# Loading the first image first, and layers 1 to 3's constants beside layer 0's first work, in a four-layer convolution and attention kernel

## The chip, the cores and the metric

The kernel runs on one core of a Trainium2 chip. A core has five engines, each with its own instruction queue: TensorE (PE in the profile; PEld is its weight load), VectorE (DVE), ScalarE (ACT), GpSimd (POOL) and SyncE (SP), which here only issues DMAs. They wait for each other through semaphores, and each engine takes its instructions strictly in the order in which they were written. The metric is the device time of one execution over a batch of 32 images, in microseconds (us). Less is better.

## The reference

Input `x` is 32 images of 56 x 56 pixels with 96 channels, float32. Four layers follow each other:

```python
# layer 0: a conditional bottleneck; rw are 4 gates per image
rw = sigmoid(mean(x, (1, 2)) @ Wr + br)
h = relu(bn(x @ einsum('be,ecm->bcm', rw, Wpw) + rw @ bpw))      # 96 -> 384 channels
h = relu(bn(sum_e rw[e] * (depthwise3x3(h, Wdw[e]) + bdw[e])))
x = bn(h @ einsum('be,emf->bmf', rw, Wpwl) + rw @ bpwl) + x      # 384 -> 96
# layer 1
x = x + depthwise5x5(x, kernel)
# layer 2
x = bn(depthwise3x3(relu(x), dw) @ pw + pw_bias)
# layer 3: shifted 7x7 window attention (3 heads) and a perceptron with gelu
x = x + attention(layernorm(x)) @ wo + bo
x = x + gelu(layernorm(x) @ w1 + b1) @ w2 + b2
```

The gates need the mean over the whole image, so nothing of layer 0 can start before its image is in SBUF, its sum is taken and the router (`rw`) has run.

## The kernel before

Line numbers are those of the kernel before, as its profile has them.

**Stages.** Each image passes four stages. `stage_router` loads the image (`xT`, 96 channels on partitions x 3136 pixels), sums it in two halves on ScalarE (`sums`, through the accumulator), makes `pooled` and `pooled_w` on VectorE, multiplies by `wr` on TensorE, and makes `rw` and the mixed weights `wmix`, `wmix2` and `mix`. `stage_conditional` is layer 0's main part: for each of four strips of 14 rows and three blocks of 128 channels it expands on TensorE, evicts on ScalarE to `h1`, and takes nine taps of the 3 x 3 depthwise convolution into `h2` (printed as `h`): the first on ScalarE, eight on VectorE, as SCALAR_TENSOR_TENSOR of 128 x 784. Then a ReLU on ScalarE, the projection on TensorE, its eviction to `y` (two buffers) on ScalarE, and the residual addition `xT <- y, xT` on GpSimd. `stage_depthwise` is layers 1 and 2 as banded matmuls with `band5`, `band3` and `pw`. `stage_swin` is layer 3.

**The order of the work.** The stages don't issue instructions. A `Recorder` notes each as a `Work` with a cost, what it waits for, and a target time. `Recorder.order` then plans the whole run with a small list of costs: at each moment a free engine takes the work with the earliest target whose inputs are ready and whose buffers (`Ring`) are free. `give` writes the instructions in that order; this is why nearly all of them carry line 488. Where TensorE would idle for longer than `SPARE_AFTER` (250 ns) and a bank is free, the planner puts in a filler: a 128 x 128 matmul of `ident` with itself (`banks<-ident` in the profile; each float32 matmul is two rows there). Image 0's and image 1's stages overlap, so the routers of both are near the start; the plan has ScalarE sum the first halves of image 0 and of image 1, and then the second halves.

**The constants.** Ahead of the planned work, written in the plain order of the program, stand:

- `scratch` (536): pieces of `h2`'s first buffer, used as room for small constants. `mhalves` (552) is one, filled with -0.5.
- `rsqrt` (557, 558): a VectorE instruction adds epsilon, and GpSimd raises to the power -0.5.
- layer 0's loads (562, 570, 583, 601), their transposition on TensorE (587, 604), and batch-norm constants `s1`, `s2`, `s3` (558, 615 to 617).
- `band5` and the six additions of `centre` to it (640), `band3`, `pw`.
- layer 2's batch norm of 128 x 96 pieces: `inv2` by `rsqrt`, then 654 and 660 to 665, which fold it into `pw`. 660 reads the bank that the matmul of 658 wrote.
- `centre_outputs` (670 to 672) for `pw` and `wo`, and 685.
- layer 3's loads, and memsets on GpSimd (699 to 712), among them the zero borders of `slots`, `kT`, `exps`, `x1`, `x2` and `h1`.

SyncE issues all of these loads before the first planned instruction, the load of image 0. In the built program each DMA issue waits for the landing of the one issued eight places before it.

Of the kernel before, what the change touches and what calls it, by code (L numbers as in the profile page):

```python
# [19 lines left out]
C = 96  # L20
CM = C + 1
M = 384
# [238 lines left out]
class Recorder:  # L261
# [77 lines left out]
    def order(self):  # L339
# [66 lines left out]
        def begin(w):  # L406
            nonlocal count
            for b in w.needs:
                if b.slot is None:
                    b.ring.free.sort()  # L410
                    b.slot = b.ring.free.pop(0)[1]
                    b.ring.begun += 1
            result.append(w)
            w.start = now
            e = w.engine
            if e == "gpsimd" or w.calls[0][0] == "scalar_tensor_tensor":
                running[e] = {"work": w, "left": w.ns, "since": now, "rate": 1.0}
                share(now)
                return
            free[e] = now + w.ns  # L420
            heapq.heappush(events, (free[e], count, None))
            heapq.heappush(events, (free[e] + w.landing, count + 1, w))
            count += 2
            if e == "tensor":
                heapq.heappush(events, (free[e] + SPARE_AFTER, count, None))
                count += 1

        left = len(self.work)
        spares = 0
        while left:  # L430
            for e in self.ENGINES:
                if free[e] > now:
# [2 lines left out]
                while queues[e]:  # L435
# [5 lines left out]
                    begin(w)  # L441
                    left -= 1
                    if e == "tensor":
                        spares = 0
                    break
                else:
                    if e == "tensor" and self.spare and now >= free[e] + SPARE_AFTER and self.spare[2].free:
                        lhs, rhs, ring = self.spare
                        w = Work(e, 0.0)
                        b = Buffer(ring)  # L450
                        operands = View(b, ring.tiles[0])[:, : rhs.shape[1]], lhs, rhs
                        w.calls.append(("matmul", operands, {"start": True, "stop": True}))
                        w.ns = cost(e, "matmul", operands, {})
                        w.needs, w.starts, w.uses, w.writes = [b], [b], [b], [b]
                        b.users[w], b.left, b.owner = True, 1, w
                        spares += 1
                        assert spares < 10000, "no work can start"
                        begin(w)
# [20 lines left out]
                count += 1  # L479
        return result  # L480

    def give(self, tc):
        with tc.manual_schedule():
            for w in self.order():
                for method, args, kw in w.calls:
                    args = [v.found() if isinstance(v, View) else v for v in args]
                    kw = {k: v.found() if isinstance(v, View) else v for k, v in kw.items()}
# [4 lines left out]
def kernel(  # L492
# [37 lines left out]
    if general:  # L530
# [2 lines left out]
        tops = ring("top", [PK, NP], 4)  # L533
        dens = ring("den", [PK, NP], 4)


    room = h2s.tiles[0].rearrange("p k n -> p (k n)")
    taken = [0]

    def scratch(rows, n):  # L540
        taken[0] += n
        return room[:rows, taken[0] - n : taken[0]]


    ident = const.tile([P, P], F32, name="ident")
# [2 lines left out]
    nc.gpsimd.memset(ones, 1.0)  # L548
    mhalf = const.tile([P, 4], F32, name="mhalf")
    nc.gpsimd.memset(mhalf, -0.5)  # L550
    mhalves = scratch(P, C)
    nc.gpsimd.memset(mhalves, -0.5)

    def rsqrt(dst, src, eps, scale=1.0):
# [75 lines left out]
    nc.vector.tensor_copy(experts[:, :, 9, :], c384[:, :, V_BPW : V_BPW + E])  # L630
    nc.vector.tensor_copy(experts[:, :, 10, :], c384[:, :, V_BDW : V_BDW + E])


    band5 = load([P, NG, 10, 32], layouts["k5"], "band5")
    centre = scratch(P, 64).rearrange("p (n c) -> p n c", n=2)
    nc.sync.dma_start(out=centre, in_=layouts["centre"])
    for g in range(NG):
        for n in range(2):
            at = 5 * n + 2
            nc.vector.tensor_tensor(band5[:, g, at], band5[:, g, at], centre[:, n], ALU.add)  # L640
    band3 = load([P, NG, 6, 32], layouts["k3"], "band3")


    pw = const.tile([C + 1, CM], F32, name="pw")
    nc.sync.dma_start(out=pw[:C, :C], in_=a["L2_conv_pw_kernel"].rearrange("a b c f -> (a b c) f"))

    def wide(name, keep=False):
        t = const.tile([P, C], F32, name=name) if keep else scratch(P, C)
        nc.sync.dma_start(out=t, in_=a[name].partition_broadcast(P))
        return t  # L650

    inv2 = wide("L2_conv_moving_var")
    rsqrt(inv2, inv2, BN_EPS)
    nc.vector.tensor_tensor(inv2, inv2, wide("L2_conv_gamma"), ALU.mult)
    dwb = scratch(C, P)
    nc.vector.tensor_scalar(dwb, ones[:C].to_broadcast([C, P]), col(U_DWB), None, ALU.mult)
    pt = mm.tiles[4]
    nc.tensor.matmul(pt[:, :C], dwb, pw[:C, :C], start=True, stop=True)
    bias2 = scratch(P, C)
    nc.vector.tensor_tensor(bias2, pt[:, :C], wide("L2_conv_pw_bias"), ALU.add)  # L660
    nc.vector.tensor_tensor(bias2, bias2, wide("L2_conv_moving_mean"), ALU.subtract)
    nc.vector.tensor_tensor(bias2, bias2, inv2, ALU.mult)
    nc.vector.tensor_tensor(bias2, bias2, wide("L2_conv_beta"), ALU.add)
    nc.vector.tensor_tensor(pw[:C, :C], pw[:C, :C], inv2[:C], ALU.mult)
    nc.vector.tensor_copy(pw[C:, :C], bias2[C : C + 1])

    def centre_outputs(w):

# [2 lines left out]
        nc.vector.tensor_scalar(mean, mean, 1.0 / C, None, ALU.mult)  # L671
        nc.vector.tensor_scalar(w[:, :C], w[:, :C], mean, None, ALU.subtract)

    centre_outputs(pw)


    wq = load([C, C], a["L3_conv_wq"], "wq")
    wk = load([C, C], a["L3_conv_wk"], "wk")
    wv = load([C, C], a["L3_conv_wv"], "wv")
    wo = const.tile([C + 1, CM], F32, name="wo")  # L680
    nc.sync.dma_start(out=wo[:C, :C], in_=a["L3_conv_wo"])
    nc.sync.dma_start(out=wo[C:, :C], in_=a["L3_conv_bo"].rearrange("(o c) -> o c", o=1))
    centre_outputs(wo)
    if not general:
        nc.vector.tensor_scalar(wo[:C], wo[:C], -1.0, None, ALU.mult)
    w1 = load([C, M], a["L3_conv_w1"], "w1")
    w2 = load([P, NB, C], a["L3_conv_w2"].rearrange("(k p) f -> p k f", p=P), "w2")
    b2 = wide("L3_conv_b2", True)
    if general:
        masks = load([PK, 2, NP * PK], layouts["mask"].rearrange("l q j k -> q l (j k)"), "masks")  # L690
    else:
        keep_last = load([P, NP, WT], layouts["keep_last"], "keep_last")
        keep_column = load([P, WT], layouts["keep_column"], "keep_column")

        slots = ring("slots", [C, NWIN, SLOT], 3)

        exps = ring("exps", [P, NH, NP, PK], 2)
        for t in slots.tiles + kTs.tiles + exps.tiles:
            nc.gpsimd.memset(t, 0.0)
        ones32 = const.tile([P, HD], F32, name="ones32")  # L700
        nc.gpsimd.memset(ones32, 1.0)

    for t in x1s.tiles + x2s.tiles + [h1.tiles[0] for h1 in h1s]:
        nc.gpsimd.memset(t, 0.0)
    for t in filtereds.tiles + oTs.tiles:
        nc.gpsimd.memset(t[C:], 1.0)

    for t in lnsqs.tiles:
        nc.gpsimd.memset(t[:, :, C:], C * LN_EPS)
    for u in (U_LN1G, U_LN2G):
        nc.vector.tensor_scalar(col(u), col(u), math.sqrt(C), None, ALU.mult)

# [12 lines left out]
    def stage_router(b):  # L728

        xT = chip.new(xTs).part(*range(NROW))  # L730
        sums = new_small("sums", [C, 2])
        chip.sync.dma_start(out=xT, in_=x[b])
        yield 3
        for q in range(2):
            part = xT[:, q * HALF * W : (q + 1) * HALF * W].part(*range(4 * q, 4 * q + 4))
# [733 lines left out]
    for step in range(B + 3):  # L1469
# [11 lines left out]
        if step < B:  # L1481
            stages.append((stage_router(step), 12, when("router", step)))
        interleave(stages)
    chip.give(tc)


def build(nc, shapes, batch):
# [41 lines left out]
```

## Time and profile before

| what | us |
|---|---|
| median of 3 runs | 5219.56 (5214.7 to 5220.35) |
| the profiled execution, its own time | 5218.23 |
| its span, first to last instruction | 5216.4 |
| TensorE busy | 5044.7 (97%) |
| VectorE busy | 4300.9 (82%) |
| images 0 and 1: DMAs issued from | 29.19 |
| first sum on image 0, on image 1 | 37.10, 41.65 |
| first router matmul | 53.08 |
| first tap on VectorE | 62.36 |
| TensorE busy from 0 to 10, 20 to 30, 30 to 40 us | 0.96, 1.60, 0.00 |
| DMA rate from 20 to 30, 30 to 40 us | 157, 251 GB/s |

The time between the profiled execution's span and its own time (1.8 us) is what lies around the first and last instruction. A line of the timeline gives the start in us from the span's start, the duration (from the first to the last where several like instructions are merged, with their count), the engine, the line, the operation and its tiles, and in brackets how long the engine was idle before and what ended that. Buffer numbers are left out of the names, so `h` stands for `h1` and `h2` alike, and for the small constants that borrow `h2`'s room. SPq lines are DMA issues, not transfers. Lines of the chain of waits give start, duration and who held the chain.

### The profile page before, as it was taken

The page shows a single profiled execution, that of the slowest core. Times are in us where ns is not written, and L with a number is a line of the kernel's source. Part 1 is how long each engine was busy: PE and PEld are TensorE (multiplying, and loading weights), DVE is VectorE, ACT ScalarE, POOL GpSimd, SP SyncE. Part 2 cuts the span into 40 slices and gives each one's busy share as a digit, 9 for nine tenths or more (in the row PEclk, how much of TensorE's full clock was granted, in tenths as well). Part 3 has the DMA queues.
Part 4 walks back from the last instruction along what each step waited for, and adds up shares of the span by engine and source line. Part 5 has one row for each costly group of instructions (what it writes and reads, how often), then busy time and mean ns, then how long its engine had stood idle before and what let it go on. Part 6 is the DMA issues. An engine that isn't in the chain of part 4 may idle for free.

```text
span 5216.4 us, 139773 instructions
## 1 busy us (share of the span) xinstructions
PE 5044.7 (97%) x58652; PEld 3347.7 (64%) x58652; DVE 4300.9 (82%) x5560; ACT 3841.3 (74%) x7649; POOL 3041.9 (58%) x2432
## 2 busy tenths in 40 slices
PE   5889999999999999999999999999999999999999
PEld 3556666666666666666666666666666666666677
DVE  6887988888988888988888888888888888898722
ACT  2457787777778777777877777877777877777755
POOL 5456755565765555666465665656566555566533
PEclk9899999999999999999999999999999999999999
DMA  1111111111111111101111111111111111110110
GB/s 43 22 27 39 23 28 33 37 36 38 31 25 31 33 39 36 39 20 29 35 37 36 38 27 27 32 36 37 37 34 23 32 33 39 36 39 20 24 28 19
DMA packets 482579, 166.35 MB, mean 32 GB/s; under 512 B 477952, under 2 KB 478613, under 8 KB 478869
## 3 DMA queue, kind: packets, MB, share of 16 engines
q1 hardware_dynamic: 481940, 157.33, 14.7%
q8 instruction: 464, 7.60, 0.6%
q14 instruction: 175, 1.43, 0.1%
HBM read 41.60 MB, written 38.54 MB: 15 GB/s over the span
## 4 chain that ended last, share of the span: by engine, by line
PE 74%; POOL 9%; DVE 6%; ACT 5%; issue 5%; DMA 1%; SPq 0%; DVEq 0%; POOLq 0%; ACTq 0%
PE banks L488 74%; DVE h L488 4%; POOL tb L488 3%; POOL lnd L488 2%; ACT exps L488 2%; POOL xT L488 2%; POOL exps L488 1%; POOL var L488 1%; ACT h L488 1%; ACT hid L488 1%; DVE hid L488 1%; DVE wmix L488 1%; DMA out<-tb 1%; ACT slots L488 0%; DVE res L488 0%
## 5 line engine op out<-in xcount | busy, mean ns | idle before, releaser
L488 DVE SCALAR_TENSOR_TENSOR h<-h,mix,h 128x784 f32<-128x784 f32 x3072 | 3309.9, 1113 | 71.7 <-ACT h L488 56.5
L488 POOL TENSOR_TENSOR var<-var,mhalf 112x4 f32<-112x4 f32 (+1 forms) x512 | 775.4, 1520 | 418.9 <-DVE var L488 409.8
L488 PE MATMUL banks<-x,band 32*32 32x392 f32 x24576 | 851.1, 508 | 0.0
L488 POOL TENSOR_TENSOR xT<-y,xT 96x392 f32<-96x392 f32 x256 | 480.6, 1879 | 491.8 <-ACT y L488 490.5
L488 PE MATMUL banks<-xT,wmix 96*128 96x448 f32 (+1 forms) x1536 | 693.7, 550 | 1.4 <-issue 1.4
L488 ACT ACTIVATE h<-h,biasd,s 128x784 f32<-128x784 f32 x384 | 399.0, 1039 | 348.8 <-DVE h L488 348.6
L488 ACT ACTIVATE hid<-banks,c 128x448 f32<-128x448 f32 (+1 forms) x768 | 437.0, 583 | 287.9 <-PE banks L488 279.5
L488 PEld LDWEIGHTS banks<-w,hid 128*112 128x112 f32 x5376 | 579.9, 182 | 82.0 <-issue 37.8
L488 POOL TENSOR_TENSOR tb<-res 112x384 f32<-112x384 f32 (+1 forms) x256 | 459.8, 1801 | 282.7 <-DMA out<-tb 181.2
L488 PE MATMUL banks<-hT,w 96*128 96x448 f32 (+1 forms) x1536 | 615.5, 502 | 0.2 <-DVE tb L488 0.2
L488 POOL TENSOR_TENSOR lnd<-res,var 112x384 f32<-112x384 f32 (+1 forms) x512 | 590.3, 1159 | 32.8 <-PE banks L488 16.2
L488 ACT ACTIVATE h<-banks,bias,s 128x448 f32<-128x448 f32 (+1 forms) x768 | 539.4, 710 | 90.8 <-PE banks L488 85.0
L488 PE MATMUL banks<-w,hid 128*112 128x96 f32 x5376 | 588.4, 266 | 7.4 <-ACT hid L488 6.4
L488 PE MATMUL banks<-h,wmix 128*96 128x392 f32 x1536 | 560.2, 503 | 17.0 <-ACT h L488 17.0
L488 PEld LDWEIGHTS banks<-x,band 32*32 32x32 f32 x24576 | 407.8, 103 | 247.0 <-issue 161.7
L488 ACT ACTIVATE exps<-banks 49x196 f32<-49x196 f32 x1536 | 507.8, 331 | 40.5 <-PE banks L488 15.8
L488 POOL TENSOR_TENSOR exps<-exps,keep_column 49x147 f32<-49x147 f32 x224 | 207.2, 925 | 479.3 <-ACT exps L488 443.8
L488 PEld LDWEIGHTS banks<-h,wmix 128*96 128x96 f32 x1536 | 245.1, 166 | 258.9 <-issue 210.3
L488 PEld LDWEIGHTS banks<-xT,wmix 96*128 96x128 f32 x1536 | 259.2, 191 | 199.8 <-issue 95.0
L488 ACT ACTIVATE h<-h,mix 128x784 f32<-128x784 f32 x384 | 364.5, 949 | 29.3 <-POOL h L488 21.1
L488 DVE TENSOR_REDUCE var<-lnsq 112x4 f32<-112x388 f32 (+1 forms) x512 | 253.1, 497 | 159.7 <-POOL lnd L488 120.0
L488 PEld LDWEIGHTS banks<-hT,w 96*128 96x128 f32 x1536 | 256.4, 190 | 144.9 <-issue 73.3
(131 smaller groups left out, 7499.6 us busy)
## 6 DMA issues: line engine op xcount, KB each, us to landing
xT<-in_x SPq DMA_DIRECT2D x32, 1176.0 KB
x<-xT SPq DMA_DIRECT2D x384, 98.0 KB
out<-tb SPq DMA_DIRECT2D x128, 168.0 KB
filtered<-x SPq DMA_DIRECT2D x384, 49.0 KB
filtered<-x SPq DMA_DIRECT2D x384, 42.0 KB
out<-tb SPq DMA_DIRECT2D x128, 126.0 KB
filtered<-x SPq DMA_DIRECT2D x384, 7.0 KB
wpw<-in_L_conv_Wpw SPq DMA_DIRECT2D x1, 576.0 KB
```

What stands on the lines that cost most here:

```text
L488: getattr(getattr(self.nc, w.engine), method)(*args, **kw)
```

## The change

- Image 0's load is written ahead of all other loads of the kernel; in the plan an entry without instructions (`brought`) stands in its place. Image 1's load stays planned, and now follows layer 0's constants and `pw`.
- The loads of layers 1 to 3 are held back. `give` writes three groups between the planned instructions, each ahead of the first instruction that the plan starts at 15, 45 or 85 us: `first_others` (18 loads, and the memsets of layers 1 to 3), `more_others` (the `rsqrt` of `inv2`) and `last_others` (the `band5` additions, layer 2's folding, `centre_outputs`).
- The small constants of layers 1 to 3, and `mhalves`, lie in the room of `x3` instead of `h2`'s first buffer. The matmul for `bias2` stays ahead; a copy now takes it out of its bank at once.
- The planner puts in no filler before the first planned matmul. 37 fillers go.

```diff
+        begun = False
...
                     if e == "tensor":
-                        spares = 0
+                        spares, begun = 0, True
...
-                    if e == "tensor" and self.spare and now >= free[e] + SPARE_AFTER and self.spare[2].free:
+                    if e == "tensor" and begun and self.spare and now >= free[e] + SPARE_AFTER and self.spare[2].free:
...
+    def brought(self, v):
+        w = Work("sync", self.target)
+        w.ns, w.landing = COST["sync", "dma_start"][0], IMAGE_LANDING
+        self.work.append(w)
+        self.touch(w, v, True)
...
-    def give(self, tc):
+    def give(self, tc, others):
+        others = sorted(others.items(), reverse=True)
         with tc.manual_schedule():
             for w in self.order():
+                while others and w.start >= others[-1][0]:
+                    others.pop()[1]()
...
+    nc.sync.dma_start(out=xTs.tiles[0], in_=x[0])
+    rooms = [h2s.tiles[0].rearrange("p k n -> p (k n)"), x3s.tiles[0].rearrange("p g m w -> p (g m w)")]
...
-    mhalves = scratch(P, C)
+    mhalves = scratch(P, C, 1)
...
+    bias2 = scratch(P, C, 1)
+    nc.vector.tensor_copy(bias2, pt[:, :C])
...
+    def first_others():
+        for t, src in held:
+            nc.sync.dma_start(out=t, in_=src)
+        if not general:
+            for t in slots.tiles + kTs.tiles + exps.tiles:
+                nc.gpsimd.memset(t, 0.0)
+            nc.gpsimd.memset(ones32, 1.0)
+        for t in x1s.tiles + x2s.tiles:
+            nc.gpsimd.memset(t, 0.0)
+        for t in filtereds.tiles + oTs.tiles:
+            nc.gpsimd.memset(t[C:], 1.0)
+        for t in lnsqs.tiles:
+            nc.gpsimd.memset(t[:, :, C:], C * LN_EPS)
+
+    def more_others():
+        rsqrt(inv2, inv2, BN_EPS)
...
+    def last_others():
+        for g in range(NG):
+            for n in range(2):
+                at = 5 * n + 2
+                nc.vector.tensor_tensor(band5[:, g, at], band5[:, g, at], centre[:, n], ALU.add)
+        nc.vector.tensor_tensor(inv2, inv2, gamma2, ALU.mult)
+        nc.vector.tensor_tensor(bias2, bias2, pwb2, ALU.add)
+        nc.vector.tensor_tensor(bias2, bias2, mean2, ALU.subtract)
+        nc.vector.tensor_tensor(bias2, bias2, inv2, ALU.mult)
+        nc.vector.tensor_tensor(bias2, bias2, beta2, ALU.add)
+        nc.vector.tensor_tensor(pw[:C, :C], pw[:C, :C], inv2[:C], ALU.mult)
+        nc.vector.tensor_copy(pw[C:, :C], bias2[C : C + 1])
+        centre_outputs(pw)
+        centre_outputs(wo)
+        if not general:
+            nc.vector.tensor_scalar(wo[:C], wo[:C], -1.0, None, ALU.mult)
+
+    others = {15000: first_others, 45000: more_others, 85000: last_others}
...
-        chip.sync.dma_start(out=xT, in_=x[b])
+        if b:
+            chip.sync.dma_start(out=xT, in_=x[b])
+        else:
+            chip.brought(xT)
...
-    chip.give(tc)
+    chip.give(tc, others)
```

In the built program of after, VectorE has the addition of epsilon to `inv2` (557 before) after the 12th tap of image 0, and `last_others` after the 49th. GpSimd has the memsets of `first_others` ahead of the power for `s1`, and the power for `inv2` behind all of these and ahead of the first residual addition. SyncE has image 0, layer 0's loads, `pw`, image 1, the 18 held loads.

## The prediction

> **What bounds the kernel now.** I read the page first (busy shares, slices), then the chain that ended last, then VectorE, ScalarE, GpSimd and SyncE in order of time over the first 340 us, where every line of the diff acts.
>
> The page says that TensorE fills the span, except in its first slice:
>
> ```profile
> span 5216.4 us, 139773 instructions
> PE 5044.7 (97%) x58652; PEld 3347.7 (64%) x58652; DVE 4300.9 (82%) x5560; ACT 3841.3 (74%) x7649; POOL 3041.9 (58%) x2432
> ```
>
> The middle of the run can't change: stripped of the fillers, TensorE's order in the two built programs is the same, and the banks differ by one fixed renaming; so are ScalarE's, VectorE's and GpSimd's orders, apart from the first 140 instructions or so. 37 fillers go. Nothing later is replanned, so a time won or lost before image 0 has filled the pipeline should arrive whole at the end.
>
> In order of time, before the first multiply-add of the depthwise taps (columns: start, duration, engine, line, operation, idle before it and what ended it):
>
> ```profile
> 13.93 0.22 SPq L583 DMA_DIRECT2D h<-in_L_conv_b  x1
> 18.74 0.36 SPq L562 DMA_DIRECT2D band<-in_k  x1
> 27.05 15.68 POOL L558 TENSOR_TENSOR h<-h 128x96 f32<-128x96 f32 x1 [1.06 <-DVE h L557]
> 29.19 0.90 SPq L488 DMA_DIRECT2D xT<-in_x  x2
> 41.65 1.51 ACT L488 ACTIVATE xT<-xT 96x1568 f32<-96x1568 f32 x1 [2.95 <-DMA xT<-in_x]
> 46.05 0.19 ACT L488 ACTIVATION_READ_ACCUMULATOR xT<-xT 96x1 f32 x1
> ...
> 42.76 0.26 DVE L654 TENSOR_TENSOR h<-h 128x96 f32<-128x96 f32 x1 [15.80 <-POOL h L558]
> 43.59 9.65 PE L488 MATMUL banks<-ident 128*128 128x128 f32 x66 [19.15 <-DVE h L660]
> 53.08 0.28 PE L488 MATMUL banks<-wr,pooled_w 96*128 96x4 f32 x2
> 53.60 0.15 DVE L488 TENSOR_TENSOR rw<-banks,br 128x4 f32<-128x4 f32 x1
> 62.36 63.71 DVE L488 SCALAR_TENSOR_TENSOR h<-h,mix,h 128x784 f32<-128x784 f32 x67
> ```
>
> Both images are issued last, at 29.19. The power of layer 2's variance holds GpSimd 15.68 us; its reader L660 holds a bank, and 33 fillers (66 rows) stand before the router's matmul until 53.08. From 62.36 VectorE is the bound: 67 taps with no pause.
>
> Then the chain, and VectorE after the 67 taps:
>
> ```profile
> 94.06 32.89 POOL xT L488
> 126.97 0.69 ACT y L488
> ```
>
> ```profile
> 134.86 15.22 DVE L488 SCALAR_TENSOR_TENSOR h<-h,mix,h 128x784 f32<-128x784 f32 x16 [8.78 <-ACT h L488]
> ```
>
> An addition on GpSimd that takes 1.0 us alone (the next three, from 126.95) lasted 32.89 us beside uninterrupted taps. ScalarE's third `y` waited for it, the following taps got no input, and VectorE stood for 8.78 us. GpSimd instructions that read get no turn inside a tight row of taps. This row decides the case, since the change puts the 15.68 us power into that row of taps.
>
> **Part 1, first image first: the second image still decides.** ScalarE's order stays: first half of image 0, first half of image 1, then the second halves. VectorE takes both sums before `rw`. So the router's start hangs on image 1, which stands behind layer 0's constants on SyncE. The ninth DMA issue waits for the first: before, the issues paused from 10.2 to 13.93 for `wpw` and `wpwl`. Now image 0 (1176 KB at the 251 GB/s of the window 30 to 40: 4.8 us) is ahead of these. Issued at 5.77, 1.9 us later its bytes move (estimate; `wpw` took about that), so it ends near 12.5 and the four `wpwl` land about 18.0 instead of 13.93: all later issues move by 4.07. Image 1 stands one DMA (`pw`, 0.45) behind the place of `band` (18.74): 18.74 + 4.07 + 0.45 = 23.3. With 1.0 to the first byte, 4.8 of bytes and 1.8 from last byte to semaphore (bytes ended at 39.8, the sum began at 41.65) it lands at 30.9 instead of 41.65: 10.75 us won. Bounds: 29.0 (no shift of 4.07, partly made up by a slower load) to 32.5 (bytes shared with the bands behind it).
>
> **Part 2, the constants moved off the router's way.** The sums take 4.59 us from image 1's landing (41.65 to 46.24), now 30.9 to 35.5; a reduction, a product (0.14, 0.28) and `rw` is at 35.9. Before, `rw` came 7.36 after the last sum, since 33 fillers were queued; now 0.4. That wins 6.95. Together 53.60 becomes 35.9, **-17.7**. Layer 0's own constants are ready in time: GpSimd's memsets (slots to `filtered`, `oT`) now stand ahead of `s1`'s power, by their rows (5.8 to 25.6 before) they end near 22; the powers (1.73 and 0.55) then end near 25.6, VectorE's rest near 26.6, 8 us before the first sum is read. The 18 held DMAs, 0.47 us each, stand behind image 1 and land before 45; nobody reads them before 90.
>
> **Part 3, fillers.** Their 9.65 us are in the 6.95 already. What they may leave is a cold TensorE: the first twenty rows of the 66 went at 213 ns, the rest at 112, and cold expansion rows took 0.75 us instead of 0.375 (3.19 us for four at 77.33, 1.67 at 68.42). Now router, 3 fillers, router, 10 fillers run without a pause for some 5 us before the expansions, longer than the 4.3 us the twenty rows took. I take 0; the bound is 4 rows, +1.5. The Trainium skill (TensorE: Matmul & The Clock Gate, Part 1) says activity of some 3.4 to 4 us releases the half rate, which agrees; by it too the sum has 0 here.
>
> **Part 4, VectorE's constant work inside the taps.** After 12 taps comes L557's sum with epsilon (0.20), after 49 taps the six band additions (0.70) and then L654 to L685's fifteen instructions (42.76 to 46.33: 3.57). Before, they lay under the wait for the image and the fillers; now they are in the bound engine's row: **+4.5**.
>
> **Part 5, the power of 96 columns.** It is queued on GpSimd after the 12th tap, some 12 us into the row. L654 follows the 49th tap, 35 us later, so on paper 15.7 are hidden in 35. But it reads, and that row of taps gave an addition nothing for 32.89 us. I take it as held until the first break, the band additions, after which VectorE stands in front of L654 for all of it: **+15.7**. The other end is 0, if it gets in after the 12th tap and needs the port only for moments. For 0 speaks a trace record: at 342.29 a power of four columns got in between two taps and the next tap lasted 1.035 us, not stretched; so it doesn't hold the port while it computes, for four columns. Nearest to our place is the row at 94.06 (same engine pair, same kind of taps), so I take the full price. The Trainium skill (SBUF — State Buffer, Who interferes with whom) has it that an instruction of VectorE with two SBUF inputs and a reading one of GpSimd lock each other out, the first for its whole duration. By that rule even an early entry would stop the taps for 15.7, and the price is the same either way; by the four-column row an early entry costs nothing. The rule speaks against the change, and the row at 94.06 is on its side.
>
> **Part 6, the 8.78 us pause.** While VectorE stands for the power, GpSimd is free; the additions queued behind it follow during the 3.57 us of small instructions. `y` number three is then released near 108, and the taps 50 to 67 (17.0 us) cover the 7.9 us that ScalarE needed from 126.97 to the next start. So the old pause is filled: **-8.8** (bounds -8.8 and 0).
>
> **Sum:** -17.7 + 4.5 + 15.7 - 8.8 = **-6.3 us**. The profiled execution took 5218.23 (span 5216.4): 5211.9. The median of the three runs is 5219.56, 1.3 above it: 5213. About 0.2% (10.4 us) is what a measurement of this kernel can tell from no change, so this is within it.
>
> **Rivals.**
> - *The power gets its port early.* Taps and power run side by side: -17.7 + 4.5 - 8.8 = -22.0; if a later addition then starves and gives a pause of 8.8 back, -13.2. For it: the four-column record, and an addition at 179.02 that got in after one tap. Against: five additions before 340 us starved 16 to 33 us. 5197 to 5206.
> - *The old pause stays behind the new one (slower).* If the four additions don't get through during the small instructions, which have two SBUF inputs too, the row of taps 50 to 67 starves them again, and the 8.78 us remain: -17.7 + 4.5 + 15.7 = +2.5; where the additions of the next strip starve once more for want of a break, another 8.8: +11.3, to 5231. It decides from the point where the taps restart before the second addition has ended. Against: three additions took 2.9 us, in 3.57.
> - *The start doesn't reach the end.* TensorE is 97% busy; if another wait before 570 us (VectorE stood 16.5 us at 346 for a matmul) has slack that swallows the gain, nothing is left: 5219. Against: that wait is on work in the same order, which comes earlier too.
>
> **How the numbers follow.** The forecast (-2 to -10): 0.66; early port (-13 to -22): 0.18; old pause stays: 0.11; no effect: 0.05. Faster by over 0.2% is the early port and the lucky end of the forecast (image 1 at 29): 0.26. Slower by over 0.2%: a third of the second rival, 0.04, and 0.02 for what I don't see: 0.06. The rest, 0.68, is within. The likeliest case's own range is 5209 to 5218. For 8 in 10 I go down to 5198, which leaves out only the early port's end, and up to 5222, which leaves out the doubled pause.
>
> **What would show it.** `rw`'s first addition near 35.9 and the first tap near 44.7; image 1's sum beginning near 30.9; one GpSimd power lasting 40 to 55 us instead of 15.7, and VectorE standing some 15 us ahead of the second small product; no 8.8 us pause after tap 67; tap 68 near 128.6 (was 134.86). I am wrong if the power lasts about 16 us with taps going on, or if a pause of 8 us or more follows tap 67.

## The result, and the profile after

The changed kernel takes 5202.26 us in the median of 7 runs (5199.32 to 5214.36), against 5220.2 for the kernel before (median of 7, beside it). The ratio is 0.9971, with a 95% interval of 0.9961 to 0.9981: 0.29% faster, 18 us. The forecast was 5213, a change inside 0.2%; the time lies in the given range of 5198 to 5222, but in the part of it that the first rival named. The profiled execution of after was one of its longer ones (5214.36), at a granted clock of 0.985 instead of the 0.987 or 0.988 of those near the median: its lead over the profile of before stays near 15 us up to some 900 us of the span (15.5 at 929) and melts slowly from there (3.9 at the last tap), so I read the start, where every line of the diff acts, and take the end from the medians.

The page of after, its span and busy shares:

```profile
span 5212.6 us, 139630 instructions
PE 5050.6 (97%) x58578; PEld 3343.9 (64%) x58578; DVE 4300.9 (83%) x5561; ACT 3836.9 (74%) x7649; POOL 3028.8 (58%) x2432
```

74 matmul rows fewer (37 fillers), and one VectorE instruction more, the copy of `bias2`. The way to the first tap, from the timelines of SyncE, ScalarE, TensorE and VectorE of after (start, duration, engine, line, operation; the planned work now has line 500):

```profile
5.63 0.32 SPq L548 DMA_DIRECT2D xT<-in_x  x1
13.34 0.27 SPq L597 DMA_DIRECT2D h<-in_L_conv_bpw  x1
23.27 0.42 SPq L500 DMA_DIRECT2D xT<-in_x  x1
31.40 1.51 ACT L500 ACTIVATE xT<-xT 96x1568 f32<-96x1568 f32 x1 [16.38 <-DMA xT<-in_x]
35.05 0.59 PE L500 MATMUL banks<-wr,pooled_w 96*128 96x4 f32 x2 [9.23 <-DVE pooled_w L500]
36.48 0.15 DVE L500 TENSOR_TENSOR rw<-banks,br 128x4 f32<-128x4 f32 x1
45.31 11.69 DVE L500 SCALAR_TENSOR_TENSOR h<-h,mix,h 128x784 f32<-128x784 f32 x12
```

Image 1 is issued at 23.27, and ScalarE, which had nothing to do for 16.38 us, begins its sum at 31.40 (41.65 before). The router's matmul waits for nothing but `pooled_w`, and the first tap is at 45.31 instead of 62.36. Then what decided the case, the 96-column power and its surroundings on GpSimd and VectorE:

```profile
56.92 0.20 DVE L571 TENSOR_SCALAR x<-x 128x96 f32<-128x96 f32 x1
57.04 35.21 DVE L500 SCALAR_TENSOR_TENSOR h<-h,mix,h 128x784 f32<-128x784 f32 x37
57.20 16.40 POOL L572 TENSOR_TENSOR x<-x 128x96 f32<-128x96 f32 x1 [31.76 <-DVE x L571]
77.26 16.83 POOL L500 TENSOR_TENSOR xT<-y,xT 96x392 f32<-96x392 f32 x2 [3.66 <-ACT y L500]
92.18 2.37 DVE L730 TENSOR_TENSOR band<-band,x 128x32 f32<-128x32 f32 x6
94.47 0.24 DVE L731 TENSOR_TENSOR x<-x 128x96 f32<-128x96 f32 x1
97.77 26.56 DVE L500 SCALAR_TENSOR_TENSOR h<-h,mix,h 128x784 f32<-128x784 f32 x28
126.29 6.52 DVE L500 SCALAR_TENSOR_TENSOR h<-h,mix,h 128x784 f32<-128x784 f32 x6 [1.96 <-POOL h L500]
155.83 35.78 POOL L500 TENSOR_TENSOR xT<-y,xT 96x392 f32<-96x392 f32 x4 [15.09 <-ACT y L500]
196.84 20.58 DVE L500 SCALAR_TENSOR_TENSOR h<-h,mix,h 128x784 f32<-128x784 f32 x21 [9.01 <-ACT h L500]
```

The power took 16.40 us beside 37 taps that took 35.21 us without a break, and L731, its reader, followed the band additions at once. The next GpSimd instruction, an addition that takes 1.0 us alone, starved for 15.9 us until the band additions, and the one at 155.83 for 32.9. The latter ends in a pause of VectorE of 9.01 us, as the kernel before had one of 8.78 after tap 67. The chain of waits has the same, start and duration:

```profile
23.27 8.12 DMA xT<-in_x
...
155.83 32.88 POOL xT L500
```

### The profile page after: what moved, and what is told of

Same layout as the page of the kernel before. It is cut to its first block, busy times and chain, and to the rows that moved or that the text cites. A ratio compares the mean times of both kernels' runs of the same rounds, so it can differ in the third digit from the quotient of the medians.

```text
span 5212.6 us, 139630 instructions
## 1 busy us (share of the span) xinstructions
PE 5050.6 (97%) x58578; PEld 3343.9 (64%) x58578; DVE 4300.9 (83%) x5561; ACT 3836.9 (74%) x7649; POOL 3028.8 (58%) x2432
## 3 DMA queue, kind: packets, MB, share of 16 engines
q1 hardware_dynamic: 481940, 157.33, 14.8%
## 4 chain that ended last, share of the span: by engine, by line
PE 74%; POOL 10%; DVE 5%; ACT 5%; issue 4%; DMA 1%; SPq 0%; ACTq 0%; DVEq 0%; POOLq 0%
PE banks L500 74%; DVE h L500 3%; POOL tb L500 3%; POOL lnd L500 2%; POOL xT L500 2%; ACT exps L500 2%; POOL exps L500 2%; POOL var L500 1%; ACT hid L500 1%; ACT h L500 1%; DMA out<-tb 1%; DVE wmix L500 1%; DVE hid L500 1%; ACT slots L500 0%; DVE res L500 0%
## 5 line engine op out<-in xcount | busy, mean ns | idle before, releaser
L500 POOL TENSOR_TENSOR tb<-res 112x384 f32<-112x384 f32 (+1 forms) x256 | 476.4, 1866 | 286.7 <-DMA out<-tb 196.7
L500 POOL TENSOR_TENSOR lnd<-res,var 112x384 f32<-112x384 f32 (+1 forms) x512 | 594.8, 1168 | 32.8 <-PE banks L500 16.2
L500 PE MATMUL banks<-h,wmix 128*96 128x392 f32 x1536 | 557.7, 501 | 15.7 <-ACT h L500 15.7
L500 ACT ACTIVATE exps<-banks 49x196 f32<-49x196 f32 x1536 | 506.2, 330 | 40.2 <-PE banks L500 15.3
L500 ACT ACTIVATE h<-h,mix 128x784 f32<-128x784 f32 x384 | 364.5, 949 | 18.0 <-POOL h L500 10.1
```

Source lines behind the costliest of these rows:

```text
L500: getattr(getattr(self.nc, w.engine), method)(*args, **kw)
```

## The experiments

The measure that I use for all runs is the **shift**: the start of a tap on VectorE minus the start of the same tap in the profile of before, both counted from the span's start. In after it is -17.1 us at the first tap, -16.8 at the 30th, -11.2 at the 50th, -20.1 at the 68th, -12.0 at the 150th and -15.1 at the 240th (some 330 us into the span of before). Gains and losses can be read off where they arise. Time is the median of a run's 4 to 10 executions minus that of the kernel before on the same chip; line numbers are those of each run's own file.

| run | first tap, us | shift at tap 30 / 50 / 68 / 150 / 240 | time against before, us | ratio and its 95% interval |
|---|---|---|---|---|
| after | 45.31 | -16.8 / -11.2 / -20.1 / -12.0 / -15.1 | -17.9 | 0.9971, 0.9961 to 0.9981 |
| e1 fillers back | 44.81 | -17.3 / -11.7 / -20.6 / -12.8 / -16.2 | -15.5 | 0.9973, 0.9962 to 0.9984 |
| e2 fillers out, nothing else | 56.41 | -6.0 / -6.0 / -6.5 / -6.5 / -6.9 | -7.1 | 0.9991, 0.9982 to 1.0001 |
| e4 power mid row | 45.05 | -17.2 / +3.4 / -5.5 / +1.6 / -1.8 | -2.0 | 1.0001, 0.9991 to 1.001 |
| e5 image 1 second | 42.22 | -19.9 / -14.3 / -23.2 / -15.3 / -16.7 | -16.2 | 0.9971, 0.9959 to 0.9982 |
| e6 held loads first | 55.45 | -6.7 / -1.1 / -9.9 / -2.2 / -3.7 | -3.8 | 0.9991, 0.9982 to 1.0001 |
| e7 second router later | 33.93 | -23.3 / -2.7 / -11.6 / -3.5 / -4.8 | -6.9 | 0.9989, 0.9979 to 0.9998 |
| e8 break later | 45.98 | -16.1 / -16.1 / -16.1 / -12.2 / -12.5 | -12.8 | 0.9979, 0.9969 to 0.9988 |
| e9 early power | 37.76 | -19.6 / -14.0 / -22.9 / -14.8 / -16.2 | -22.3 | 0.9959, 0.9945 to 0.9973 |
| e10 three breaks | 46.04 | -16.1 / -13.8 / -22.6 / -18.0 / -19.5 | -21.5 | 0.9956, 0.9939 to 0.9972 |
| e11 all three | 35.07 | -22.3 / -20.0 / -28.9 / -24.5 / -26.2 | -29.9 | 0.9944, 0.9930 to 0.9957 |
| e12 after again | 45.37 | -16.7 / -11.2 / -20.0 / -12.1 / -13.5 | -17.6 | 0.9968, 0.9957 to 0.9979 |

The last shift and the time agree: over eleven of these twelve rows they differ by 0.1 to 4.1 us, and in e9 by 6.1. What the first 330 us win does arrive at the end; the third rival ("the start doesn't reach the end") is out.

### e1 and e2: the fillers

e1 is after, with the fillers ahead of the first planned matmul put back; e2 is the kernel before, without them.

```diff
-        begun = False
+        begun = True
```

> The changed kernel with its 37 fillers put back ahead of the router's matmul; nothing else. Theory (image 1's landing decides in the changed kernel): the 33 fillers behind the matmul for bias2 start near 26 us and take the 9.65 us that they took before, so they end near 35.5, when the router's first product is ready at 34.9. The first tap moves from 45.3 by 0 to +1, the time by 0 to +1 us: no difference. Rival (the fillers are part of the gain, as the 6.95 us of my part 2 has it): the first tap 5 to 7 us later, near 51, and the time 5 to 7 us longer.

> The kernel before, without fillers ahead of the router's matmul; nothing else of the change. Theory (before, the fillers stood between the sums and the router): the second router product no longer waits until 53.4, rw comes near 46.9 instead of 53.6 and the first tap near 55.7 to 57 instead of 62.36 (up to 1.5 for a cold TensorE); the time falls by 5 to 7 us. Rival (only the image's landing matters): the first tap stays within 1 us of 62.4.

TensorE and VectorE of e1:

```profile
35.43 0.28 PE L500 MATMUL banks<-wr,pooled_w 96*128 96x4 f32 x2
...
44.81 11.69 DVE L500 SCALAR_TENSOR_TENSOR h<-h,mix,h 128x784 f32<-128x784 f32 x12
```

With 66 filler rows back in after, the router is at 35.43 (35.05 without them) and the first tap 0.5 us earlier, since image 1's sum happened to begin at 30.89 instead of 31.40. In the kernel before, taking them out moves the first tap by 6.0 us (56.41), and the pause after tap 67 stays (8.22 us). So the fillers cost some 6 us only where L660 held them back to 43.59. In after the matmul for `bias2` is early, its bank is copied out at once, and the 66 rows run from 26.11 on, while image 1 is still awaited. Of the 6.95 us that Part 2 booked as 33 fillers, taking them out wins 6.0 by itself (e2), and with the bank freed early they cost nothing (e1).

### e3 and e4: the power in its place, and in the middle of the row

e3 replaces the power by an addition of -0.5, in the same place (layer 2's scale is then another number). e4 keeps the power but hands it its input through a copy on ScalarE some ten taps later, in the middle of the row.

```diff
 def more_others():
-    rsqrt(inv2, inv2, BN_EPS)
+    nc.vector.tensor_scalar(inv2, inv2, 1.0, BN_EPS, ALU.mult, ALU.add)
+    nc.gpsimd.tensor_tensor(inv2, inv2, mhalves, ALU.add)          # e3
...
+def power():                                                        # e4, at 60 us of the plan
+    nc.scalar.copy(plus_eps, inv2)
+    nc.gpsimd.tensor_tensor(inv2, plus_eps, mhalves, ALU.pow)
...
+    others = {15000: first_others, 45000: more_others, 60000: power, 85000: last_others}   # e4
```

> The changed kernel with GpSimd adding -0.5 where it took the power -0.5 of layer 2's variance (the power is left out, so layer 2's scale is another); same place, same 128 x 96 tile, same two inputs. In the changed kernel the power got in at the first boundary between two taps (57.2 us, the next tap 1160 ns instead of 1021). Theory by place (what arrives just behind the small VectorE instruction gets in): the addition gets in too, within 1 us, and lasts under 1.5 us. Theory by kind (a power gets in where an addition starves): the addition lasts until the band additions, some 35 us. Either way the first residual addition at 77 us still starves until 92 to 93, since its own place is unchanged.

> The changed kernel, with the power's input handed over by ScalarE (a 128 x 96 copy, 0.3 us) some 10 taps later, so that the power starts in the middle of an unbroken row of taps, near 66 us, with no small VectorE instruction before it. Theory by place: it starves until the band additions near 92 us, VectorE then stands 15 us in front of the fold of inv2, and the time is 10 to 16 us longer than the changed kernel's. Theory by kind (a power reads its 192 numbers in a burst of 0.14 us and gets in at a boundary): it lasts 16 to 17 us from its start, one tap is stretched by 0.1 to 0.2 us, the first residual addition waits behind it, and the time is that of the changed kernel within 2 us. Theory by moment (whether a reading instruction gets in depends on when within a tap it asks): either, by the moment at which the copy ends.

GpSimd of e3; then GpSimd and VectorE of e4:

```profile
57.10 1.11 POOL L718 TENSOR_TENSOR x<-x 128x96 f32<-128x96 f32 x1 [31.29 <-DVE x L717]
```

```profile
66.06 41.33 POOL L723 TENSOR_TENSOR x<-x 128x96 f32<-128x96 f32 x1 [40.61 <-ACT x L722]
91.78 0.88 DVE L736 TENSOR_TENSOR band<-band,x 128x32 f32<-128x32 f32 x6
107.43 1.06 DVE L737 TENSOR_TENSOR x<-x 128x96 f32<-128x96 f32 x1 [14.77 <-POOL x L723]
```

e3 has no row in the table: of it there is one execution (5209.5 us). In it a plain addition in the power's place gets in as quickly as the power did, and the residual addition of after starves in the same way 20 us later. So it isn't the kind of instruction that decides. e4 is the forecast as I had written it: the power starves from 66.06 to the band additions at 91.78, so 25.7 of its 41.33 us are waiting and the rest is its work; VectorE stands for 14.77 us ahead of its reader, and the shift at tap 50 is +3.4, 14.6 worse than after's -11.2. The whole gain is gone (ratio 1.0001).

### e5 and e6: what the router waits for

e5 issues image 1 directly behind image 0, ahead of the constants; e6 issues the 18 held loads ahead of image 1.

```diff
+    for n in range(2):                                              # e5
+        nc.sync.dma_start(out=xTs.tiles[n], in_=x[n])
...
-        if b:
+        if b > 1:
...
-    others = {15000: first_others, 45000: more_others, 85000: last_others}
+    others = {0: first_others, 45000: more_others, 85000: last_others}    # e6
```

> Image 1's load is written directly behind image 0's, ahead of layer 0's constants. Theory (the first tap hangs on the later of image 1's sums and layer 0's own constants): image 1's 1.2 MB then lie ahead of the constants, which slip by about 4.8 us, so that VectorE's constant work ends near 31 instead of 26.2 and now decides instead of image 1 (sums done near 23): rw near 32.5 to 33 (after: 36.48), first tap near 41 to 42 (after: 45.31), the time 3 to 5 us below that of after, some 20 to 23 us below before. Rival (TensorE, ScalarE or the expansions' own weights limit the start, and not the landing of image 1): first tap stays within 1 us of 45.3, no change against after. Second rival (the constants slip by more than image 1 gains, since the issue queue waits for landings): first tap after 47, time 2 us or more above after.

> The 18 held loads of layers 1 to 3 are issued ahead of image 1's load, as they were in the kernel before; image 0 stays first. Theory (image 1's landing decides, image 0's does not): image 1 is issued some 8 us later, its sum begins near 39 to 40 (after: 31.40), rw near 44.5, first tap near 53 (after: 45.31), and the time is about 8 us above that of after, some 10 below before. Rival (image 0's early landing is what pays): first tap stays near 45.3, time as after.

e6: image 1 is issued at 33.72 instead of 23.27, its sum begins at 41.34, the first tap is at 55.45, 10.1 us later than in after, and at tap 240 it is 11.3 behind; against before, the time is 14 us worse than after's. The direction is the theory's; I had said 8 us, and the held loads took 10.5 since their issues wait for landings too. Image 1's landing decides in after, and image 0's, whose sum begins 18 us ahead of it, is worth nothing by itself: e6 wins 6.9 us at the first tap, about what the fillers alone do (6.0 in e2). e5: the sum on image 1 begins at 18.60, `rw` at 30.17 now stands behind layer 0's constants, and the first tap is at 42.22, 3.1 us earlier, as expected; at tap 240 1.6 are left, and the time, expected 3 to 5 us below after's, can't be told from it (0.9971 twice).

### e7: image 1's router out of the way, and the power again

The router of image 1 (all but its load) is written as one block behind the first strip's evictions.

```diff
+            late = [w for w in works if w.second and w.engine != 'sync' and w.start < SECOND_AT]
+            rest = [w for w in works if not (w.second and w.engine != 'sync' and w.start < SECOND_AT)]
+            at = next(n for n, w in enumerate(rest) if w.start >= SECOND_AT)
+            for w in rest[:at] + late + rest[at:]:
...
```

> The router of image 1 (its sums, pooled, rw and mixed weights, not its load) is written as a block behind the first strip's evictions instead of beside image 0's router; everything else as in after. Theory (image 0's router waits only because it is written behind work on image 1): rw of image 0 near 27 to 28, right behind layer 0's constants, first tap near 36 (after: 45.31), then about 4 us of image 1's router in VectorE's row, so tap 30 near 5 us earlier than in after; the time 3 to 6 us below after, if the gain arrives. Rival (the block in the row costs what it wins, or gives the power and the additions another moment to arrive, so that a pause of 8 to 15 us comes back): time the same as after or up to 10 above.

GpSimd and VectorE of e7:

```profile
50.55 0.20 DVE L579 TENSOR_SCALAR x<-x 128x96 f32<-128x96 f32 x1
50.67 35.08 DVE L508 SCALAR_TENSOR_TENSOR h<-h,mix,h 128x784 f32<-128x784 f32 x37
50.83 50.46 POOL L580 TENSOR_TENSOR x<-x 128x96 f32<-128x96 f32 x1 [25.00 <-DVE x L579]
85.66 0.89 DVE L738 TENSOR_TENSOR band<-band,x 128x32 f32<-128x32 f32 x6
101.32 1.06 DVE L739 TENSOR_TENSOR x<-x 128x96 f32<-128x96 f32 x1 [14.77 <-POOL x L580]
```

The first tap is 11.4 us earlier than in after, the 30th 6.5. Then the power, in the same place behind the same small instruction, starves for 37 taps (34.8 us, from 50.83 to the band additions at 85.66; the expectation of e9 says 34), VectorE stands for 14.77 us, and against before the kernel is 11 us worse than after. That is the rival, and the end of an idea that I held after e3 and e4: that a reading instruction gets in if it arrives right behind a small VectorE instruction. In six programs with the power there (after in both its profiles, e1, e5, e6, e8, e10) it got in, as did e3's addition; in this one it did not. In the records the only difference that I find is where in the running tap GpSimd's instruction begins: 163 to 170 ns after the tap's start where it got in, 161 ns in e7. Whether these 2 ns are the cause isn't shown. Shown is only that the same place behind the same small instruction doesn't ensure an early entry, and no line of the diff was written to ensure it.

### e8 and e10: where the row is broken

e8 moves the third group from tap 49 to tap 77. e10 splits it: band additions behind tap 49, folding behind 107, centrings behind 128.

```diff
-    others = {15000: first_others, 45000: more_others, 85000: last_others}
+    others = {15000: first_others, 45000: more_others, 115000: last_others}                             # e8
+    others = {15000: first_others, 45000: more_others, 85000: last_others, 150000: fold, 172000: centring}   # e10
```

> The third group (band additions, layer 2's folding) is written at 115 instead of 85 us of the plan, behind some 77 taps instead of 49; all else as in after. Theory (the small VectorE instructions after tap 49 are what lets the starved first residual addition in, and so what removes the old pause): the addition that starts near 77 lasts over 30 us instead of 16.83, VectorE stands 7 to 9 us after tap 67, tap 68 near 118 (after: about 114.5), and 5.6 us more go into the row behind it: the time 4 to 9 us above after. Rival (the pause went because the row as a whole lies otherwise, or the additions get in by themselves): the addition lasts 17 us or less, no pause over 3 us after tap 67, tap 68 near 109 to 110, and the time as after.

> As after, but the third group is split: the band additions stay behind tap 49, layer 2's folding (7 small instructions) goes behind tap 107, the two centrings (7) behind tap 128. Theory (a starved residual addition gets in where small VectorE instructions break the row, and the pause of 9.01 us that after has near 188 us is the old one given back): the addition that starts near 155 us lasts under 6 us instead of 33, VectorE's pause near 188 us is under 3 us, the shift against the kernel before is -19 to -21 at tap 150 (after: -12.0) and -19 to -22 at 330 us, the time 4 to 7 us below that of after. Rival (the pauses of VectorE are not what sets the end by then: TensorE or ScalarE is): the pause goes, but the shift at 330 us is -15 to -17 as in after, and the time is the same. Second rival (breaks don't let the additions in): pause and time as in after.

GpSimd and VectorE of e8, then of e10:

```profile
77.92 35.80 POOL L500 TENSOR_TENSOR xT<-y,xT 96x392 f32<-96x392 f32 x4 [3.65 <-ACT y L500]
118.72 9.55 DVE L500 SCALAR_TENSOR_TENSOR h<-h,mix,h 128x784 f32<-128x784 f32 x10 [8.78 <-ACT h L500]
```

```profile
153.28 3.92 POOL L500 TENSOR_TENSOR xT<-y,xT 96x392 f32<-96x392 f32 x2 [15.09 <-ACT y L500]
155.38 0.95 DVE L735 TENSOR_TENSOR x<-x 128x96 f32<-128x96 f32 x1
156.36 0.95 DVE L736 TENSOR_TENSOR x<-x 128x96 f32<-128x96 f32 x1
```

Without the small instructions at tap 49 the old pause is back, 8.78 us to the hundredth, with the 68th tap at 118.72. With small instructions at tap 107 the second starved addition gets in at once (two of them in 3.92 us; VectorE's L735 and the next, L736, are stretched to 0.95 us each, from 0.26 and 0.25), the pause of 9.01 us at 188 is gone, and the shift at tap 150 is -18.0 instead of -12.0. So small VectorE instructions are what lets a starved reader in. What a pause is worth is less plain: e10 has the pause of 9.01 us no longer, and of it 6.0 us are left at tap 150 and 4.4 at tap 240, since its stretched instructions and longer waits near tap 160 take the rest. e8 has one such pause and after has one, 72 taps further on: that is why e8 is only 1.0 to 2.5 us behind the two profiles of after at tap 240 (its median is 5 above, with intervals that overlap).

### e9, e11 and e12: the power out of the row, all three edits, and after again

e9 is e7 with layer 2's variance loaded before image 1, and its power ahead of the taps. e11 has the edits of e7, e9 and e10 together, with the epsilon behind the mixed weights. e12 is after without any edit, beside e11.

```diff
+    inv2 = scratch(P, C, 1)
+    nc.sync.dma_start(out=inv2, in_=a["L2_conv_moving_var"].partition_broadcast(P))
...
-    inv2 = wide("L2_conv_moving_var")
...
+    others = {15000: first_others, 30000: more_others, 85000: last_others, 150000: fold, 172000: centring}   # e11
```

> As the run with image 1's router written later (e7), but layer 2's variance is loaded with layer 0's constants, and its epsilon and power stand ahead of the taps, on a GpSimd that is idle from 26 us on. Theory (all that e7 lost against after is its power, starved over 34 taps for 50.46 us, which made VectorE stand 14.77 us): the power starts near 27, before the row of taps, and lasts about 16 us beside the first taps; VectorE doesn't stand ahead of the second small product; the shift against the kernel before stays near -23 at tap 30 (e7: -23.3), near -18 at tap 49 (e7: -2.7; after: -11.2), and near -21 at 330 us (after: -15.1); the time 4 to 7 us below that of after. Rival (the start's gain doesn't arrive, since image 1's router now lies in the row or the later additions starve longer): the shift at 330 us no better than -16, the time as after or above. Second rival (the power, begun before the row, is interrupted by the row and starves too): it lasts over 40 us, and the time is that of e7.

> Image 1's router behind the first strip's evictions (as e7), layer 2's power ahead of the taps (as e9, but with its epsilon behind the mixed weights, so that VectorE doesn't wait for that load ahead of them), and the third group in three pieces behind taps 49, 107 and 128 (as e10). Theory (each of the three pays where it did alone, and e9's expansions were slow, 7.96 us for 12 rows instead of 4.39, only because TensorE stood 0.64 us ahead of them): expansions 4.4 us, first tap near 34, the shift against the kernel before -23 at tap 30, -21 near tap 60, near -25 at 330 us; the time 24 to 28 us below before and 6 to 10 below after. Rival (what is won ahead of 340 us beyond some 20 us is lost again in waits of that stretch): shift at 330 us no better than -20, the time as e9 and e10, some 22 below before. Second rival (an addition or the power starves in a new place): a pause of 8 us or more in VectorE, the time as after.

> The changed kernel once more, without any edit, on the chip of the run beside it. Theory (the power gets in at the first end of a tap in this program because the row around it is the same each time): the power lasts 16.40 us again, VectorE pauses 9.0 us near 188, the time 15 to 20 us below before. Rival (whether it gets in is chance from one execution to the next): the profile has it starved for 40 us or more, or the times fall into two groups some 13 us apart.

GpSimd and TensorE of e9 and, in the second fence, of e11:

```profile
28.22 15.67 POOL L580 TENSOR_TENSOR x<-x 128x96 f32<-128x96 f32 x1 [2.14 <-DVE x L579]
31.43 7.96 PE L508 MATMUL banks<-xT,wmix 96*128 96x448 f32 x12 [0.64 <-DVE wmix L508]
```

```profile
30.53 15.68 POOL L580 TENSOR_TENSOR x<-x 128x96 f32<-128x96 f32 x1 [4.50 <-DVE x L579]
30.54 4.90 PE L508 MATMUL banks<-xT,wmix 96*128 96x448 f32 x12
```

Begun before the row, the power runs 15.7 us beside VectorE's work, and no tap beside it is stretched (1029 to 1035 ns) in either run; e7's stand of 14.77 us is gone, and the later additions starve as in after. e9 missed part of its expected lead by another way: its first tap is at 37.76 instead of e7's 33.93, because VectorE waited for the early load (1.20 us), TensorE then stood 0.64 us ahead of the expansions, and these took 7.96 us instead of 4.39, so that VectorE's wait ahead of the first tap grew from 3.80 to 5.79 us. With the epsilon moved behind the mixed weights (e11) there is no such wait and they take 4.90. e11 is the fastest kernel of the study: 5191.02 us, 0.9944 (0.9930 to 0.9957) of before, and 12 us below after on the same chip (5203.31; the two intervals meet at 0.9957). The expected first tap was 34, it came at 35.07; the shifts are within about 1 us of the expectation, and the time 2 us better. e12 repeats after: the power lasts 16.40 us, the pause is there (8.80 us), and its times (5193.90 to 5209.76) follow the granted clock, 0.990 for the shortest, 0.986 for the three longest, and don't form two groups some 13 us apart. One thing differs from the first profile of after: image 1's sum began 0.5 us earlier (30.90), but the 20 filler rows ahead of the expansions took 4.54 us instead of 3.21 and held them back, and the first tap came no earlier (45.37).

## Why the prediction was right or wrong

- **Part 1, image 1 decides: right.** Its sum was forecast for 30.9 and began at 31.40; its issue for 23.3, at 23.27. e6 shows that this landing, not image 0's, sets the start.
- **Part 2, the constants off the way: right.** `rw` at 36.48 (35.9), first tap at 45.31 (44.7): -17.05 for -17.7. The constants of layer 0 were ready 8.4 us early (8). The 6.95 us booked as fillers belong to two edits at once, as e1 and e2 show.
- **Part 3, cold TensorE at 0: right in the profile of after** (12 expansion rows 4.47 us, as before). In e12, the same program, slow filler rows cost some 0.5 us, and the bound of +1.5 was too small: in e9 the expansions took 3.6 us longer than in e7, of which 2.0 arrived at the first tap.
- **Part 4, constant work in the row: +4.5 forecast, +5.6 measured** (shift -16.8 to -11.2), and 0.1 for the sum with epsilon. The six band additions took 2.37 us instead of 0.70, because the starved residual addition got its turn beside them.
- **Part 5, the power +15.7: wrong; this is the step that failed.** I took the power "as held until the first break". It got in at the first end of a tap and cost VectorE 0.13 us: the 14th tap lasted 1160 ns, the 13th 1031. The mechanism and the price exist, as e4 and e7 show (14.77 us each), but not at this moment of arrival. The record of the four-column power, which I had set aside for the addition at 94.06, told rightly that a power doesn't stop the taps while it computes, and that it may get in. With 0.1 in place of 15.7 the sum is -21.9, the rival's -22.0 but for this 0.1.
- **Part 6, the old pause -8.8: right in size, wrong in its way, and only put off.** The pause after tap 67 went (shift -11.2 to -20.1) because the band additions let the first residual addition in, not because VectorE stood. But a later addition starved and gave 9.01 us back before tap 150, the case that the first rival named at -13.2. Up to tap 240 VectorE's pauses of over 0.6 us sum to 23.1 us in before and 19.8 in after, so little of the 8.8 was won for good. The profiles of after have -15.1 and -13.5 at tap 240, the medians -17.9 and -17.6.
- **The sum, term by term.** From the forecast of -6.3 to the -15.1 at tap 240: +0.7 for the start, +1.2 for the constant work, -15.6 for the power, -0.1 for the old pause, and +5.0 between taps 68 and 240, which the sum had at nothing. That the time lies in the range is partly luck: the forecast's own case reached only from 5209 to 5218, and the range was drawn down to 5198 to take in most of the rival's.
- **The chances.** I gave the early entry 0.18 and the starved one 0.66. Starved rows were the more frequent in the trace of before, but they were additions, and the one row of the same kind, the four-column power, spoke the other way. With the power in this place six programs of seven went against me; they are near copies of one another, so this is no frequency, but the early entry deserved at least an even chance.
- **The other rivals.** "The old pause stays behind the new one" needs VectorE to stand for the power first. It did so in e4 and e7, and there too the pause after tap 67 went (from tap 50 to tap 68 the shift falls by 8.9 us in both), so that rival is out. "The start doesn't reach the end" is refuted by all runs.

The Trainium skill (SBUF — State Buffer, SBUF: two separate sides) has whichever starts first, a VectorE instruction with two SBUF inputs or a GpSimd one that reads SBUF, hold the shared port pair for the whole instruction. Here a power of 16.40 us lengthened one tap by 0.13, in the profile of after, and left the 16 behind it as they were; by the rule the taps would have stood still for as long as it ran. Where the two differ, the run decides.

## What to carry to other kernels

A GpSimd instruction that reads SBUF and is queued beside a tight row of two-input VectorE instructions can wait for the whole row, and what decides whether it does is open; price it at both ends, and then move it so that it starts before the row, where it stretched no tap (e9, e11). A starved GpSimd reader was let in by six or seven small VectorE instructions: put constant work that has to be done anyway behind the arrival of the readers that someone waits for (e10). And look at what the first instruction of a queue really waits for: here the first image's router stood behind work on the second image, and moving that by itself moved the first tap by 11.4 us (e7).

## What the runs showed of the hardware that was not expected

- A GpSimd power of 96 columns costs VectorE 0.13 us of its 16.40; an addition of the same size in its place (e3) does the same in 1.11 us. The wait is all in getting the first turn: 0.9 us (end of the running tap), or 25.7 us in e4 and 34.8 in e7 (until the row breaks); the 41.33 and 50.46 us of their rows are this wait and the work.
- That wait has two outcomes with nothing between them in seven programs with the same instruction in the same place: 163 to 170 ns into a tap it got in at the next end, at 161 ns it missed 36 ends of taps in a row. Other readers in the same traces show no simple threshold: additions got in that began 11 to 25 ns into a tap, and starved at 52 (e8), 184 (before) and 216 to 244 ns. That a reader loses every time, and not now and then, would fit a row of taps with a constant step; this was not tried, and what decides stays open.
- TensorE's expansions went at 0.66 us a row in e9 behind a gap of 0.64 us, and at 0.37 in e7 without it. The profile's granted clock says 1.00 in both. The windows of e9, with length, busy time (and instructions) of PE, PEld, DVE, ACT and POOL, granted clock, DMA share and GB/s:

```profile
30.00:34.00 4.00, 3.36 (x8) 1.95 (x8) 1.97 (x6) 0.64 (x1) 4.00 (x1) 1.00 0.95 254
34.00:40.00 6.00, 6.00 (x16) 3.19 (x16) 2.17 (x3) 4.12 (x7) 6.00 (x1) 1.00 0.51 128
```

In e9 the 20 filler rows before the gap took 4.53 us, and the rows stayed slow until 38.5, 7.1 us behind the gap. In e11 the same rows took 4.53 us too, no gap followed, and the expansions took 4.90. So a gap may put the change to the fast rate off; no run measured that alone. The moment moves without a gap as well, as the starts of TensorE's rows show: some 3.7 us after the work began in after and 6.4 in e12, the same program. Behind the change a gap of 0.53 us cost nothing (4.47, in after). The clock column shows none of this. The Trainium skill (TensorE: Matmul & The Clock Gate, Part 1) has the rate rise after at least one window of some 3.4 us of sustained work; the 3.7 of after is near one such window, the 6.4 of e12 near two.
